# Attention of an audio tower: token tiles of 128 rows, and the last 64 tokens of two heads in one tile

## The chip, the cores and the metric

The kernel runs on one core of one Trainium2 chip. The metric is the device time of one execution in microseconds. Engines are named as in the profile: PE is TensorE (matrix products), PEld its weight loads, DVE is VectorE, ACT is ScalarE, POOL is GpSimd, and SP is the engine that issues the transfers.

## What is computed

Thirty-two sounds of 160,000 samples are cut into S = 313 frames of 512 samples. A discrete cosine transform gives the tokens h. One attention layer and one feed-forward layer follow, each with a normalisation ahead of it and a residual sum behind it. Everything is float32.

```python
h = einsum('bfh,kh->bfk', frames, D)
h = h + attn(layernorm(h))
h = h + ffn(layernorm(h))

def attn(X):                                   # H = 8 heads of 64
    Q = xpos(einsum('bsd,hde->bhse', X, W_Q), False)
    K = xpos(einsum('bsd,hde->bhse', X, W_K), True)
    V = einsum('bsd,hde->bhse', X, W_V)
    p = softmax(einsum('bhse,bhte->bhst', Q, K)) * Dmat      # Dmat = gamma_h ** |s - t|
    Y = einsum('bhst,bhte->bhse', p, V)
    Yn = group_norm(Y) * gn_weight + gn_bias                 # over each head's 64 values
    return silu(X @ W_G) * Yn @ W_O

def ffn(x):                                    # N = 256 units
    theta = x[..., None, :] / (1 + abs(W)) + B_param         # b, s, N, 512
    sin, cos = sine and cosine of theta, rounded to 4096 steps of the circle
    return silu(sum(cos * attn_cos) @ proj_cos.T + sum(sin * attn_sin) @ proj_sin.T)
```

The feed-forward layer takes a sine and a cosine of 32 x 313 x 256 x 512 angles each, which makes up most of the kernel.

## The kernel before

**Feed-forward.** Work goes in rounds of 32 units for a ring of up to 16 sequences. A slot holds 24 (sequence, unit, chunk of 128 features) pieces of 313 tokens, 7512 columns. For each slot DVE makes table indices (L665), adds a quarter turn (L674) and masks (L681); ACT takes two sines of 128x7512 (L689), each into one of two `trig` buffers; PE sums each of them over the features with 24 products against one-hot weights (L711), 32 output rows at a time. In the trace a float32 product leaves two records. The ring grows over the kernel: sequences join it at the rounds in `STARTS`, two at a time, so their attention has to be finished by then. At the beginning and the end the ring is narrow.

**Attention.** `attention()` computes one sequence. Its 313 tokens are cut into three tiles of N = 105 rows, which start every 104 rows (`ROW0` = 0, 104, 208), so neighbouring tiles share one token. The shared row of V is set to zero once (L362) so that it isn't counted twice. The steps, in order:
- `rows` (L296 to L308): a product of tokens with a 512x512 matrix, tokens as output rows. For each of four chunks `c` of the features three products, one for each row tile, into three banks of `W` in PSUM. It is used for the cosine transform, V, the output matrix, and once in `output` (L595).
- `layernorm`, then `transposed` (L285 to L294): 4 x 3 transposes on PE.
- `rotary` (L367): q and k of a pair of heads, by `columns` (L310), then L384 and L387 on DVE.
- `scores` (L391): for a pair of heads three row tiles; each has a product for either head (64 rows of contraction, 105 output rows, 313 columns, L401), the row maximum (L406) and the difference from it (L410) on DVE. The two products use different halves of the array's rows.
- the exponential on ACT (L427) in two halves of four heads, 4 x 3 x 313 = 3756 columns each, and its row sums on DVE (L442). For sequences 0, 1 and three more, when the ring is narrow, ACT does 24 exponentials of 313 columns, which sum their rows themselves (L431).
- per head: nine transposes of 105x105 (L457) into three banks, and the product with the decay on DVE (L469, 3 x 313 columns), with a decay table loaded for each head (L450) into one of the two halves of `u`. After every second head three pairs of products with V (L480; two heads in the two halves of the array's columns), and a copy (L486).
- the gate (L490 to L495), the sums of squares of each head (L515), the group norm's factor (L522 to L527, transposed in L532 and copied in L535), spread over the 64 features of a head by a product with `head_w` (L540), the output matrix and the second normalisation.

Sequences 0 and 1 run at the very start, side by side in two sets of buffers, `a` and `b`, and nothing else runs then. The other 30 run one after the other in `a`, between the feed-forward slots.

**What sets the order.** `Plan` (L52) takes every step with a key (when it is due), an engine, an assumed duration in ns, and what it reads and writes; `emit` walks through assumed time and, on each engine, takes the ready step of the lowest key. The program is emitted in that order, and each engine runs its own instructions in order. So a step that waits on PE holds up the feed-forward products behind it. Assumed durations that matter here: 970 for a product of `rows`, 400 for three transposes, 690 for a pair of score products, 610 for a product of the group norm.

**Buffers.** `prob` holds eight heads of three tiles (24 x 313 columns). Before the scores are in it, parts of it hold the table of the rotation, its products and other short-lived things; `W` has four banks.

## Time and profile before

| what | us |
|---|---|
| time, median of 3 runs | 18446.96 (18434.6 to 18453.94) |
| time of the profiled execution | 18427.45 |
| its span, first to last instruction | 18425.7 |
| mean granted TensorE clock | 0.924 |
| L689, 2758 sines | 17390.1 busy, 6391 ns each |
| L711, 131072 records | 10255.2 busy |
| L665, L681, L674 together | 15015.5 busy |
| L427, 54 exponentials of 105x3756 | 177.1 busy, 3327 ns each |
| L303 and its weight loads, 2160 + 840 records in `a` | 1436.0 and 482.8 busy |

A group of the profile gives the line, the engine and the operation, then what it writes and reads with the shape, how often it occurs, its busy time and the mean length of one. The time after the second bar is how long the engine stood idle just before instructions of the group, and what ended that. Records of PE overlap, so a mean length is longer than the pace; the pace is read from the timeline, where each stretch of equal instructions has a start, a length and a number.

### The profile page before, as it was taken

Reading aid. Unit: us, or ns where it says so; the run is one execution under the profiler, and the core shown is the slowest. Engines: PE = TensorE matmul, PEld = TensorE weight load, DVE = VectorE, ACT = ScalarE, POOL = GpSimd, SP = SyncE. Lnnn points to the kernel's source line nnn. Section 1 sums busy time; section 2 is a strip of 40 time slices with the busy share of each in tenths; the row PEclk is TensorE's granted clock in tenths of the full one; section 3 lists DMA queues with packets and bytes.
Section 4 is the critical chain, followed back from the end, with each engine's and each line's share of the span. In section 5 each row is a group of like instructions: output and inputs, shape, how many; then the busy total and the mean of one; then the engine's idle time right before and its main releaser. Section 6 shows DMA issues by size and latency. Waiting matters only on the chain. (4 is left out here: it accounts for less than half of the span.)

```text
span 18425.7 us, 322107 instructions
## 1 busy us (share of the span) xinstructions
PE 14166.8 (77%) x146432; PEld 6345.6 (34%) x146432; DVE 17099.8 (93%) x11554; ACT 17817.6 (97%) x3250; POOL 1268.7 (7%) x1118
## 2 busy tenths in 40 slices
PE   7888888777777787777787777877777777766666
PEld 4333334333333333333333333333333333322222
DVE  6999999999999999999999999999998999988888
ACT  4899999999999999999999999999999999999999
POOL 0011111010100010000101000010100000000000
PEclk8999999999999999999999999999999999998888
DMA  3221121111111111111111111111111111110101
GB/s 95 79 67 60 56 67 58 54 48 58 49 39 48 58 50 51 52 44 54 49 56 48 50 46 50 57 51 54 45 43 49 42 52 52 42 43 22 38 26 57
DMA packets 610376, 947.69 MB, mean 51 GB/s; under 512 B 123600, under 2 KB 348880, under 8 KB 598768
## 3 DMA queue, kind: packets, MB, share of 16 engines
q1 hardware_dynamic: 609008, 927.08, 16.4%
q8 instruction: 1148, 18.81, 0.4%
q14 instruction: 220, 1.80, 0.0%
HBM read 822.15 MB, written 104.66 MB: 50 GB/s over the span
## 5 line engine op out<-in xcount | busy, mean ns | idle before, releaser
L689 ACT ACTIVATE trig<-ix 128x7512 f32<-128x7512 int16 (+1 forms) x2758 | 17390.1, 6391 | 319.2 <-PE pa L711 178.8
L711 PE MATMUL pa<-trig,hot 128*32 128x313 f32 x131072 | 10255.2, 466 | 3630.8 <-ACT trig L689 3584.3
L711 PEld LDWEIGHTS pa<-trig,hot 128*32 128x32 f32 x131072 | 4274.7, 118 | 9500.3 <-ACT trig L689 4888.7
L665 DVE TENSOR_SCALAR ix<-xT,f 128x2504 int16<-128x2504 f32 (+3 forms) x5504 | 6531.3, 1247 | 120.0 <-ACT trig L689 58.8
L681 DVE TENSOR_SCALAR ix<-ix 128x15024 int16<-128x15024 int16 (+4 forms) x1655 | 5581.6, 3387 | 39.9
L674 DVE TENSOR_SCALAR ix<-ix 128x7512 int16<-128x7512 int16 (+1 forms) x1379 | 2902.6, 2105 | 646.2 <-ACT trig L689 558.7
L318 PE MATMUL a_W<-a_xnT,a_ring 128*128 128x313 f32 x4896 | 1455.8, 440 | 56.0 <-DVE a_prob L410 13.6
L303 PE MATMUL a_W<-a_ring,a_u 128*105 128x512 f32 x2160 | 1036.6, 618 | 93.4 <-ACT a_h L599 37.6
L318 PEld LDWEIGHTS a_W<-a_xnT,a_ring 128*128 128x128 f32 x4896 | 884.0, 190 | 631.9 <-issue 252.0
L250 POOL TENSOR_TENSOR a_gu<-a_gr 105x24 f32<-105x24 f32 x90 | 118.7, 1318 | 8753.3 <-DVE a_gr L238 8748.6
L303 PEld LDWEIGHTS a_W<-a_ring,a_u 128*105 128x105 f32 x2160 | 347.6, 174 | 661.4 <-issue 567.9
L250 POOL TENSOR_TENSOR a_lu<-a_lr 105x3 f32<-105x3 f32 x180 | 196.2, 1090 | 4870.7 <-DVE a_lr L238 4861.3
L457 PE MATMUL a_W<-ident,a_prob 105*105 105x105 f32 x2232 | 294.3, 276 | 194.7 <-DVE a_prob L469 155.1
L303 PE MATMUL a_W<-a_ring,a_xnT 128*105 128x512 f32 x840 | 399.4, 614 | 16.7 <-ACT a_h L599 6.5
L457 PEld LDWEIGHTS a_W<-ident,a_prob 105*105 105x105 f32 x2232 | 242.0, 180 | 338.5 <-DVE a_prob L469 147.9
L410 DVE TENSOR_TENSOR a_prob<-a_W,a_mx 105x626 f32<-105x626 f32 x372 | 301.2, 810 | 59.7 <-PE a_W L401 36.1
L406 DVE TENSOR_REDUCE a_mx<-a_W 105x2 f32<-105x626 f32 x372 | 298.4, 802 | 43.0 <-PE a_W L401 31.8
L401 PE MATMUL a_W<-a_u 64*105 64x313 f32 x1488 | 260.9, 457 | 80.7 <-DVE a_mx L406 56.3
L469 DVE TENSOR_TENSOR a_prob<-a_W,a_u 105x939 f32<-105x939 f32 x248 | 280.0, 1129 | 25.0 <-PE a_W L457 22.6
L480 PE MATMUL a_W<-a_prob,a_h 105*64 105x313 f32 x1488 | 241.9, 453 | 76.2 <-DVE a_prob L469 76.1
L384 DVE TENSOR_TENSOR a_prob<-a_W,a_prob 128x1252 f32<-128x1252 f32 x124 | 180.7, 1458 | 49.0 <-PE a_W L380 34.5
L442 DVE TENSOR_REDUCE a_sm<-a_prob 105x6 f32<-105x1878 f32 x108 | 220.3, 2101 | 0.0
(144 smaller groups left out, 3452.3 us busy)
## 6 DMA issues: line engine op xcount, KB each, us to landing
hot<-in_hot SPq DMA_DIRECT2D x1376, 128.0 KB
xT<-xT_d SPq DMA_DIRECT2D x80, 1252.0 KB
a_u<-in_decay SPq DMA_DIRECT2D x248, 260.5 KB
xT<-xT_d SPq DMA_DIRECT2D x36, 939.0 KB
a_ring<-in_proj SPq DMA_DIRECT2D x128, 256.0 KB
a_ring<-in_dct SPq DMA_DIRECT2D x124, 256.0 KB
a_ring<-wv_d SPq DMA_DIRECT2D x124, 256.0 KB
a_ring<-in_wq SPq DMA_DIRECT2D x124, 256.0 KB
```

Of the source, the lines that this page charges most:

```text
L250: nc.gpsimd.tensor_tensor(u, r, r, ALU.mult)
L303: lambda c=c, i=i, k=k, to=to: nc.tensor.matmul(x.W[:N, to, :], lhsT[:, c, ROW0[i] : ROW0[i] + N], x.ring[k], start=(c == 0), stop=(c == N ...
L318: lambda c=c: nc.tensor.matmul(x.W[:, bank, :S], w[:, c, :], x.xnT[:, c, :], start=(c == 0), stop=(c == NC4 - 1)),
L406: lambda b=b, m=m: nc.vector.tensor_reduce(m[:N], x.W[:N, b : b + 2, :S], AX.X, ALU.max),
L410: lambda i=i, b=b, m=m: nc.vector.tensor_tensor(x.prob[:N, 2 * g : 2 * g + 2, i, :], x.W[:N, b : b + 2, :S], m[:N].unsqueeze(2).to_broadca ...
L457: nc.tensor.transpose(x.W[:N, jj, ROW0[i] : ROW0[i] + N], x.prob[:N, a, i, ROW0[j] : ROW0[j] + N], ident[:N, :N],)
L469: nc.vector.tensor_tensor(x.prob[:N, a], x.W[:N, :NT, :S], w3, ALU.mult)
L665: nc.vector.tensor_scalar(ix[:, x[0], pt * r * S : (pt + 1) * r * S], now["xT", y][:, : r * S], f[:, 0, n : n + 1], f[:, 1, n : n + 1], AL ...
L674: nc.vector.tensor_scalar(ix[:, x[1], :E], ix[:, x[0], :E], float(LUT // 4), None, ALU.add)
L681: nc.vector.tensor_scalar(ix[:, i, :E], ix[:, i, :E], LUT - 1, LUT // 2, ALU.bitwise_and, ALU.bitwise_xor)
L689: nc.scalar.activation(tl[:, :E], ix[:, x[1 - k], :E], AF.Sin, bias=-PI32, scale=ANG)
L711: nc.tensor.matmul(now["pa", p][g * 32 : g * 32 + 32, :S], now["hot", hot[n // 4 * 4, c]][:, n % 4, k, :], now["trig", w][:, s0 : s0 + S], ...
```

## The change

The row tiles become two of 128 rows and one of 64: rows 0 to 127, 128 to 255 and 249 to 312. The last one starts at S - 64, so its first seven rows (`TWICE`) are tokens that the second tile has as well. In everything that has a token in each row, the third tile's 64 rows are computed twice, in the partitions 0 to 63 and 64 to 127. In what belongs to heads, the lower half belongs to the first head of a pair and the upper half to the second. A pair of heads thus has five tiles (two full ones per head, one shared) of 313 columns, where it had six.

- `rows` issues two products of 64 columns for the third tile; `transposed` a transpose of 64 rows. The residual is loaded in four parts, and so is the one in `output`.
- `scores` does two rounds for each pair, and `last_scores` one round for two pairs.
- The exponential covers 2 x 5 x 313 = 3130 columns for each half, and 20 single ones instead of 24 where ACT sums. The row sums are five of 4 x 313 columns instead of four of 6 x 313.
- In the heads, a decay table is loaded for a pair (1195 columns instead of 521 for a head), into `u` for even pairs and into a new place, `spare`, for odd ones. Two blocks of three transposes for each head fill two banks. The last 64 columns of both heads go to a third bank, by products with the identity (`both`). The decay is multiplied in three steps for a pair: 2, 2 and 1 times 313 columns.
- The third of the products with V uses 64 rows of contraction. L515's third tile has two groups of products, and the group norm's factor is spread with three products for each `c` instead of one.
- The scratch places within `prob` move: the rotation's table is in `spare`.

```diff
+LAST = 64
...
-    STEP = (S - 1) // NT
-    N = S - STEP * (NT - 1)
-    ROW0 = [i * STEP for i in range(NT)]
+    N = P
+    ROW0 = [0, P, S - LAST]
+    TWICE = 2 * P - ROW0[2]
+    WIN = S + P
...
+            wide = sb("prob", (5 * NC4 + 4) * S)
+            self.prob = wide[:, : 5 * NC4 * S].rearrange("p (g x s) -> p g x s", g=NC4, s=S)
+            spare = wide[:, 5 * NC4 * S :]
+            self.dec = [self.u.rearrange("p c s -> p (c s)")[:, : 2 * WIN + S],
+                        spare[:, : 2 * WIN + S]]
...
                 for i in range(NT):
+                    n = P if i < 2 else LAST
                     nc.tensor.transpose(
-                        x.W[:, c, ROW0[i] : ROW0[i] + N], x.h[:N, i, c * P : (c + 1) * P],
-                        ident[:N, :N],
+                        x.W[:, c, ROW0[i] : ROW0[i] + n], x.h[:n, i, c * P : (c + 1) * P],
+                        ident[:n, :n],
...
+                def go(c=c, i=i, k=k, to=to):
+                    for o in (0,) if i < 2 else (0, LAST):
+                        n = P if i < 2 else LAST
+                        nc.tensor.matmul(
+                            x.W[o : o + n, to, :], lhsT[:, c, ROW0[i] : ROW0[i] + n], x.ring[k],
+                            start=(c == 0), stop=(c == NC4 - 1))
+                plan.add(key, "PE", 970, go, (*r, x.k("ring", k)), x.banks(to))
...
+            for p0 in (0, LAST):
+                nc.gpsimd.memset(x.v[p0 : p0 + TWICE, 2], 0.0)
...
-            for i in range(NT):
-                b = (g * NT + i) % 2 * 2
+            for i in range(2):
+                b = turns[0] % 2 * 2
...
+        def last_scores(g):
+            key, b = step(), turns[0] % 2 * 2
+            def go():
+                for y in range(2):
+                    for a in range(2):
+                        r = slice(a * DH, a * DH + DH)
+                        nc.tensor.matmul(x.W[r, b + y, :S], x.qk[y][r, 0, ROW0[2] : S],
+                                         x.qk[y][r, 1, :], start=True, stop=True)
+            plan.add(key, "PE", 1240, go, us, x.banks(b, b + 1))
+            below_max(key, b, x.prob[:, g : g + 2, 4, :], (probs[g][4], probs[g + 1][4]))
...
+                    nc.scalar.activation(x.prob[:, g0 : g0 + 2], x.prob[:, g0 : g0 + 2], AF.Exp)
...
+            plan.add(key, "SP", DMA_NS,
+                     lambda g=g, dec=dec: nc.sync.dma_start(dec, t["decay"][g]), (), kd)
...
+            for a in range(2):
+                if a:
+                    key = step("head")
+                for jj in range(2):
+                    def go(g=g, a=a, jj=jj):
+                        k = slice((1 - jj) * P, (2 - jj) * P)
+                        for i in range(2):
+                            nc.tensor.transpose(x.W[:, jj, i * P : (i + 1) * P],
+                                                x.prob[:, g, 2 * i + a, k], ident)
+                        r = slice(a * LAST, a * LAST + LAST)
+                        nc.tensor.transpose(x.W[:, jj, ROW0[2] : S], x.prob[r, g, 4, k],
+                                            ident[r, r])
+                    plan.add(key, "PE", 400, go, [probs[g][y] for y in (a, 2 + a, 4)], x.banks(jj))
+                if a == 0:
+                    def both(g=g):
+                        k = slice(ROW0[2], S)
+                        for a in range(2):
+                            r = slice(a * LAST, a * LAST + LAST)
+                            for i in range(2):
+                                nc.tensor.matmul(
+                                    x.W[r, 2, i * P : (i + 1) * P], x.prob[:, g, 2 * i + a, k],
+                                    ident, start=True, stop=True)
+                            nc.tensor.matmul(x.W[r, 2, ROW0[2] : S], x.prob[r, g, 4, k],
+                                             ident[r, r], start=True, stop=True)
+                    plan.add(key, "PE", 600, both, probs[g], x.banks(2))
+                decayed(key, 2, x.prob[:, g, a : a + 3 : 2, :], 0, a * WIN, x.banks(0, 1),
+                        (probs[g][a], probs[g][a + 2]))
+            decayed(key, 1, x.prob[:, g, 4:5, :], 2, 2 * WIN, x.banks(2), (probs[g][4],))
...
+                        f = slice(b * DH, (b + 1) * DH)
+                        r = f if jj == 2 else slice(0, P)
+                        nc.tensor.matmul(
+                            x.W[f, 3, :S], x.v[r, jj, g, f],
+                            x.prob[r, g, 4 if jj == 2 else 2 * jj + b, :],
+                            start=(jj == 0), stop=(jj == NT - 1))
...
+            def spread(c=c):
+                nc.tensor.matmul(x.W[:, c, : 2 * P], x.head_w[:, 0, c, :], x.rT[:, : 2 * P],
+                                 start=True, stop=True)
+                for b in range(2):
+                    f = slice(b * DH, (b + 1) * DH)
+                    nc.tensor.matmul(x.W[f, c, ROW0[2] : S], x.head_w[:, 1, c, f],
+                                     x.rT[:, 2 * P + b * LAST : 2 * P + (b + 1) * LAST],
+                                     start=True, stop=True)
+            plan.add(key, "PE", 610, spread, probs[1], x.banks(c))
```

## The prediction

> **What bounds the kernel now.** I read the busy shares first, then busy time in stretches, then what the busiest engine waited for.
>
> ```profile
> PE 14166.8 (77%) x146432; PEld 6345.6 (34%) x146432; DVE 17099.8 (93%) x11554; ACT 17817.6 (97%) x3250; POOL 1268.7 (7%) x1118
> ```
>
> ScalarE works 97% of the span, so 608 us of it are idle. The stretches (columns: length, then busy time of PE, PEld, DVE, ACT, POOL) say where:
>
> ```profile
> 0.00:620.00 620.00, 476.69 (x3145) 244.42 (x3149) 448.79 (x609) 326.31 (x220) 22.21 (x43) 0.87 0.30 90
> 620.00:1240.00 620.00, 508.04 (x4743) 245.33 (x4739) 585.47 (x614) 557.56 (x197) 38.84 (x53) 0.92 0.25 74
> 1860.00:2480.00 620.00, 493.38 (x4976) 235.95 (x4969) 600.01 (x442) 584.39 (x103) 52.10 (x37) 0.93 0.18 56
> ...
> 6200.00:6820.00 620.00, 499.89 (x5161) 226.18 (x5155) 590.59 (x360) 617.44 (x103) 66.89 (x50) 0.93 0.15 48
> ```
>
> Four regimes. Until 306 us (the first L689 sine) only two attentions run, in a chain of PE, DVE and ACT. From there to about 3720 us DVE is the fullest engine (585 and 600 of 620). From 3720 us ACT is full (617 of 620). After 16120 us no attention runs. Nine sequences fall into the second regime (three before 1240 us, six after), 21 into the third, by the starts of L362, one per sequence. What ACT waited for:
>
> ```profile
> ACT trig L689 <- PE pa L711: 178.8, 101, 6.1
> ACT trig L689 <- DVE ix L681: 75.9, 33, 10.5
> ```
>
> By stretch, the wait for PE is 81 us in 300 to 1240, 47 us in 1240 to 3720, 40 us in 3720 to 17200. It is a sine that finds both `trig` buffers still being read by L711.
>
> The groups that the change touches:
>
> ```profile
> L410 DVE TENSOR_TENSOR a_prob<-a_W,a_mx 105x626 f32<-105x626 f32 x372 | 301.2, 810 | 59.7 <-PE a_W L401 36.1
> L406 DVE TENSOR_REDUCE a_mx<-a_W 105x2 f32<-105x626 f32 x372 | 298.4, 802 | 43.0 <-PE a_W L401 31.8
> L457 PE MATMUL a_W<-ident,a_prob 105*105 105x105 f32 x2232 | 294.3, 276 | 194.7 <-DVE a_prob L469 155.1
> L469 DVE TENSOR_TENSOR a_prob<-a_W,a_u 105x939 f32<-105x939 f32 x248 | 280.0, 1129 | 25.0 <-PE a_W L457 22.6
> L442 DVE TENSOR_REDUCE a_sm<-a_prob 105x6 f32<-105x1878 f32 x108 | 220.3, 2101 | 0.0
> ```
>
> **Two rules of the Trainium skill.** "TensorEngine Tiling (Array Packing)", Key Properties, says that work on separate parts of the array runs side by side, but that "Changing tiling mode (not just tile) drains the TensorE". The trace agrees, in PE's timeline of the start-up (start, length):
>
> ```profile
> 80.95 1.22 PE L380 MATMUL a_W<-a_prob,swap_m 128*128 128x313 f32 x4
> 82.00 2.80 PE L318 MATMUL b_W<-b_xnT,b_ring 128*128 128x313 f32 x10
> 84.73 1.30 PE L401 MATMUL a_W<-a_u 64*105 64x313 f32 x8
> 85.97 1.32 PE L380 MATMUL b_W<-b_prob,swap_m 128*128 128x313 f32 x4
> ```
>
> Inside one mode L380 takes 1.05 us for 4 records, 0.2625 each (every product leaves two). Ten L318 then fill 2.63 us, but L401 starts after 2.73; its eight half-array records, two at a time, fill 1.05, but L380 starts after 1.24. Out and back costs 0.1 + 0.19 = 0.29 us. I go by this number; the page gives none.
> "ScalarE: Activation LUTs", What ACT_TABLE_LOAD costs, prices an activation at 186 ns plus 0.833 ns per element: 3315 ns for L427's 3756 elements. The trace has 3327; the slope holds.
>
> **ACT.** L427 goes from 3756 to 3130 elements: 626 x 0.833 = 0.52 us, 54 times, 28 us; the 21 late sequences have 42 of them, 22 us, on the path, since ACT is full there. The five sequences whose exponentials are single activations go from 24 to 20, 0.45 us apart in the timeline: 1.8 us each.
>
> **DVE, per sequence.** L406 and L410 run 10 times for 12: 2 x (802 + 810) = 3.2 us. A row of n elements costs about 145 + 1.042 n ns (from L442). L442 becomes five of 1252, 1.45 us each, for four of 2.10: 1.15 us less. L469 becomes eight of 626 (0.81) and four of 313 (0.48), 8.4 for 9.0: 0.6 us less. L535 grows by 0.07. Together 4.9 us, or 3.8 where L442 doesn't run. In the second regime that is 3 x 3.8 + 6 x 4.9 = 41 us, at most what the time there falls by. Later DVE waits for ACT anyway, and it is worth nothing.
>
> **PE, per sequence.** The products are as many as before where one half tile stands for two heads, but they change mode far more often.
> - L303: the third row tile becomes two 64-column products side by side, no longer than the one they replace, with one trip out and back for each `c`: 4 x 4 calls (L595 among them) x 0.29 = 4.6 us.
> - L290: the third transpose has 64 rows: 4 x 2 calls, 2.3 us.
> - L457: 48 transposes for 72 at 0.12 us (nine in 1.08 us): 2.9 less; 16 trips: 4.6 more.
> - The 64-column blocks of `both` are products and not transposes: for each pair four of 128 columns (0.2 us: 0.525 x 128/313), two small ones and four changes of mode, 1.85 us: 7.4 in all.
> - L540 gets 4 trips, 1.2; L515 four more products, 0.5.
> Sum: 4.6 + 2.3 + 1.7 + 7.4 + 1.7, some 18 us more on 112. Low end 13 (trips at 0.2). High end 25: trips at 0.35, and half-row products into one bank (`last_scores`, the third Y product), which no row shows, not running side by side, 4 us.
>
> **Who pays.** An ACT sine takes 6.4 us and its L711 group 3.37, so about 3 us lie between groups for attention. Along the emitted order, with these prices, the gaps that hold more than 3 us go from 45 to 52 in the stretch from 300 us, from 56 to 76 from 1240 us, and from 43 to 123 from 3720 us; what they hold above 3 us goes from 80 to 103, 67 to 102 and 49 to 167 us: 176 us more. Such an excess needn't stop ACT: with two `trig` buffers PE may fall 3 us behind, and catches up in the next short gap. The mean excess from 3720 us on is 1.4 us, so only runs of long gaps count. Bounds: none of it, or as much as before, where ACT waited about 0.8 us for each us of excess. I take 0.2: 37 us, mostly where products of L303 follow each other.
> A `both` or transpose that waits for DVE holds up the L711 group behind it, and so ACT; that wait exists now (L457 for L469, 155 us) and there are as many hand-overs as before.
>
> **Start-up** (all on the path). From 86.1 to 116.8 us twelve rounds of L401, L406, L410 take 30.7 us, 2.56 each. Ten of them save 5.1, twice: 10 us. The four fewer activations save 2. The rows (6 calls x 1.16) cost 7, L290 (4 calls, some at half clock) 5; in the heads from 182 to 212 us PE is about 85% busy with six pairs: 2.1 x 6 x 0.8 = 10; the first two pairs 1, L540 and L515 3. Net +14 us; between +3 and +25.
>
> **Moves priced at nothing.** The decay loads are four of 612 KB for eight of 260 KB. The one into `u` waits for the pair two before; a whole pair lies between. If that cover failed, a few us per pair would be lost: the 626 KB load of the frames was late by at most 6.2 us. SP has four issues fewer and two more (a residual and an output row block each in two parts), and the DMA engines are 16% busy with its queue. The two POOL memsets replace one, on an engine 7% busy.
>
> **Sum.** Profiled execution: 18427.45 us, span 18425.7; the median of the runs is 18446.96, 19.5 above. Start-up +14; DVE's 41 at 80%, since PE and ACT share that regime, -33; ACT -22; late PE +37. Net -4 us: 18423 profiled, about 18443 for the median. No change. The measurement can tell about 0.2%, 37 us.
>
> **Rivals.**
> - *The gain comes through.* The drains hide in PE's waits for ACT (3056 us from 700 to 17000), no sine waits longer: start-up +3, -41, -22: -60, so 18387. For it: from 3720 us ACT runs without a break for tens of sines. Against it: PE is already the engine that ACT waits for most.
> - *PE becomes the late engine.* In the gaps between L711 groups the changes of mode push PE behind, and ACT loses 0.8 us per us of excess as before: 176 x 0.8 = 141, +14, -63: +92, 18540. For it: the early stretches have PE at 82% already, and `both` comes in one block. It decides once half of the 176 us reach ACT: 88 + 14 - 63 = 39, over 0.2%. Against it: the second buffer.
> - *Fewer tiles aren't less work*: nothing of DVE's saving shows, since ACT paces everything: +14 - 22 + 37 = +29, 18476. It lies inside the first case's range, 18410 to 18485.
>
> **Chances.** No change 0.37 (with the last rival; 0.28 of it within 0.2%, 0.05 faster, 0.04 slower), gain 0.31 (0.29 faster, 0.02 within), PE late 0.32 (0.31 slower, 0.01 within). Faster 0.34, same 0.31, slower 0.35. The range reaches into both others: 18365 to 18550; the likeliest's own is 18410 to 18485.
>
> **What would show it.** L427 near 2.8 us; L442's successor 1.45 us; DVE busy down by about 150 us (31 x 4.9); PE busy up by 400 to 800 us, with gaps around the half-array products; the first sine near 320 us; ACT's wait for L711 from 179 to about 215 us. If that wait stays, the gain is there; if it passes 270, PE decides. Wrong altogether: a decay load that DVE waits for, or a mode change dearer than 0.35 us.

## The result, and the profile after

The changed kernel takes 18555.19 us (median of 5 runs, 18533.01 to 18563.57) against 18446.96 before: the ratio is 1.0057, with a 95% interval of 1.0043 to 1.0072. It is slower by 108 us, where no change was forecast, and 5 us above the range. Its profiled execution took 18546.98 us with a span of 18545.2, 119.5 more than before.

The sizes of the work came out nearly as forecast. The line of busy times after:

```profile
PE 14649.4 (79%) x148992; PEld 6440.8 (35%) x148992; DVE 16942.9 (91%) x11581; ACT 17788.7 (96%) x3210; POOL 1267.1 (7%) x1150
```

DVE has 157 us less, ACT 29 less, PE 483 more, 15.1 for each of the 32 sequences. The groups (L404 and L407 are L406 and L410 of before, L454 is L427, L471 is L442, L492 is L469, L502 and L505 are L457, L514 and L517 are `both`):

```profile
L407 DVE TENSOR_TENSOR a_prob<-a_W,a_mx 128x626 f32<-128x626 f32 x310 | 250.9, 809 | 71.2 <-PE a_W L436 37.4 <-PE a_W L422 25.1
L404 DVE TENSOR_REDUCE a_mx<-a_W 128x2 f32<-128x626 f32 x310 | 248.4, 801 | 32.7 <-PE a_W L436 25.7 <-PE a_W L422 6.3
L502 PE MATMUL a_W<-ident,a_prob 128*128 128x128 f32 x992 | 236.9, 324 | 213.3 <-DVE a_prob L492 198.8 <-ACT a_prob L454 13.7 <-DVE a_h L537 0.6
L514 PE MATMUL a_W<-ident,a_prob 128*64 128x128 f32 x992 | 163.6, 288 | 4.1 <-DVE a_h L537 4.1
L471 DVE TENSOR_REDUCE a_sm<-a_prob 128x4 f32<-128x1252 f32 x108 | 151.5, 1448 | 0.0
L454 ACT ACTIVATE a_prob<-a_prob 128x3130 f32<-128x3130 f32 x54 | 149.0, 2807 | 0.3
L505 PE MATMUL a_W<-ident,a_prob 64*128 64x64 f32 x496 | 143.0, 288 | 0.0
L492 DVE TENSOR_TENSOR a_prob<-a_W,a_prob 128x626 f32<-128x626 f32 x124 | 99.6, 803 | 5.7 <-PE a_W L505 4.8 <-PE a_W L517 0.8
```

128 rows cost DVE what 105 did (801 and 809 ns), and each exponential is 0.52 us shorter. The four stretches, with the columns of before:

```profile
0.00:620.00 620.00, 503.74 (x3153) 242.10 (x3157) 406.85 (x570) 297.97 (x193) 23.45 (x36) 0.86 0.29 87
620.00:1240.00 620.00, 527.60 (x4791) 242.60 (x4791) 574.59 (x627) 543.19 (x178) 54.04 (x64) 0.94 0.26 78
1860.00:2480.00 620.00, 515.31 (x5101) 240.66 (x5093) 589.81 (x441) 583.32 (x102) 59.39 (x40) 0.94 0.19 57
6200.00:6820.00 620.00, 499.30 (x5080) 218.00 (x5078) 575.82 (x356) 605.99 (x103) 61.51 (x50) 0.93 0.16 50
```

In the last of them ACT, which was full with 617 us, has 606. ACT's waits in the whole execution (L749 is the sine, L771 the products that read `trig`):

```profile
ACT trig L749 <- PE pa L771: 240.0, 138, 6.0
ACT trig L749 <- issue: 104.5, 45, 8.5
ACT trig L749 <- DVE ix L741: 69.3, 25, 14.3
```

The first row was 178.8 us. The second, 54.2 before, belongs with it: in the places looked at below, the sine starts right after a late group of L771, and the view names no releaser. The two together went from 233 to 345 us.

Both kernels take the same 2758 sines, so the starts of equal sines (counted from 0), after minus before, say where the time came from. The first is 21.0 us late; the 100th (1064 us in the kernel before) 34.2; the 491st (3734 us) 31.5; the 2400th (16107 us) 114.9. So 21 us lie in the start-up; 10 in the regime where DVE was fullest, where 33 us of gain had been forecast; and 83 in the late one, where the forecast had 22 us of gain and at most 37 of loss. In the late one, from 3734 to 16200 us, ACT's idle time ahead of sines (gaps over 0.3 us), its stalls, went from 65.6 to 162.0 us.

Between the first and the 491st sine DVE works 40 us less, as forecast, but is idle for 50 us more. The largest new wait is that of the copy behind the heads, for which the view names the products of `both` ahead of it on PE. In that stretch it is 12 us before and 38 after. The rows of the whole execution, before and after:

```profile
L486 DVE COPY a_h<-a_W 128x313 f32<-128x313 f32 x124 | 59.6, 481 | 56.9 <-PE a_W L457 47.1 <-PE a_W L318 8.2 <-PE a_W L480 1.3
L537 DVE COPY a_h<-a_W 128x313 f32<-128x313 f32 x124 | 59.9, 483 | 162.6 <-PE a_W L517 148.3 <-PE a_W L322 9.0 <-PE a_W L505 3.1
```

Three of PE's waits in the late stretch (from 3817 to 16200 us), out of a longer list:

```profile
PE a_W L502 <- DVE a_prob L492: 127.6, 55, 8.0
PE a_W L309 <- DMA a_u<-in_frames: 44.3, 9, 6.0
PE a_W L586 <- POOL a_gr L257: 31.8, 11, 4.2
```

The same three were 71.0, 21.3 and 25.9 us before. How such a wait reaches ACT is seen in the timeline of after (start, length, then the instructions; the time in brackets is the wait ahead):

```profile
12247.55 0.80 PE L586 MATMUL a_W<-ident,a_gr 128*8 128x128 f32 x3 [4.10 <-POOL a_gr L257]
12248.99 1.22 PE L594 MATMUL a_W<-a_prob 8*128 8x256 f32 x2 [0.64 <-DVE a_prob L589]
12250.13 0.48 PE L598 MATMUL a_W<-a_prob 8*64 8x64 f32 x4
12250.54 1.22 PE L594 MATMUL a_W<-a_prob 8*128 8x256 f32 x2
12252.09 6.14 PE L771 MATMUL pa<-trig,hot 128*32 128x313 f32 x48
12258.16 0.69 PE L594 MATMUL a_W<-a_prob 8*128 8x256 f32 x2
12258.36 6.47 ACT L749 ACTIVATE trig<-ix 128x7512 f32<-128x7512 int16 x1 [5.63 <-issue]
```

After 4.10 us of waiting PE runs at about half pace: L594 takes 1.22 us there and 0.69 later, the group of L771 6.14 us instead of 3.37. Two of the four spread steps (L594 and L598, with their changes of mode 3.1 us together) stand ahead of that group, and ACT stops for 5.63 us. In the kernel before, the same place has a wait of 2.52 us, one product ahead of the group, and ACT doesn't stop:

```profile
12155.59 0.43 PE L532 MATMUL a_W<-ident,a_gr 105*8 105x105 f32 x3 [2.52 <-POOL a_gr L253]
12156.59 0.79 PE L540 MATMUL a_W<-a_prob 8*128 8x313 f32 x2 [0.57 <-DVE a_prob L535]
12157.31 5.06 PE L711 MATMUL pa<-trig,hot 128*32 128x313 f32 x48
```

The trace also records the clock that PE was granted. It is half of full speed from 12247.5 to 12257.7 us after, and from 12158.2 to 12161.6 before. The Trainium skill ("TensorE: Matmul & The Clock Gate", Part 1) puts the half clock behind an idle window of about 3.4 us. The wait of 4.10 us agrees; before, the waits of 2.52 and 0.57 us with products between them were enough. The price is that of these timelines: 5.06 and 6.14 us for 3.37.

How much of the loss goes with this half clock? From 3734 to 16200 us it holds for 1635 us before and 1707 after, so there is hardly more of it. But 64 of the 66 us of stalls before, and 156 of the 162 after, come when more than 2 of the 14 us ahead of the sine were at half clock, which is so for 40% of all sines there. In the other twelve kernels below, it is 85 to 100% of the stalls. And the time in which PE worked for the attention at half clock went from 69 to 155 us. So the added work seems to stop ACT where it meets the half clock. No run changes the clock alone, so that is a reading of the traces and not shown by experiment.

### The profile page after: what moved, and what is told of

Read it like the earlier page. It is cut to its first block, busy times and chain, and to the rows that moved or that the text cites. A ratio compares the mean times of both kernels' runs of the same rounds, so it can differ in the third digit from the quotient of the medians.

```text
span 18545.2 us, 327113 instructions
## 1 busy us (share of the span) xinstructions
PE 14649.4 (79%) x148992; PEld 6440.8 (35%) x148992; DVE 16942.9 (91%) x11581; ACT 17788.7 (96%) x3210; POOL 1267.1 (7%) x1150
## 3 DMA queue, kind: packets, MB, share of 16 engines
q1 hardware_dynamic: 595632, 946.67, 16.7%
## 5 line engine op out<-in xcount | busy, mean ns | idle before, releaser
L749 ACT ACTIVATE trig<-ix 128x7512 f32<-128x7512 int16 (+1 forms) x2758 | 17398.6, 6392 | 438.9 <-PE pa L771 240.0
L771 PE MATMUL pa<-trig,hot 128*32 128x313 f32 x131072 | 10240.5, 466 | 3212.4 <-ACT trig L749 3156.8
L771 PEld LDWEIGHTS pa<-trig,hot 128*32 128x32 f32 x131072 | 4273.3, 118 | 9044.8 <-ACT trig L749 4355.4
L309 PE MATMUL a_W<-a_ring,a_u 128*64 128x512 f32 (+1 forms) x2880 | 1120.8, 635 | 117.5 <-DMA a_u<-in_frames 48.2
L309 PEld LDWEIGHTS a_W<-a_ring,a_u 128*64 128x64 f32 (+1 forms) x2880 | 320.0, 165 | 788.2 <-issue 675.7
L254 POOL TENSOR_TENSOR a_lu<-a_lr 128x3 f32<-128x3 f32 x180 | 201.5, 1119 | 4970.1 <-DVE a_lr L242 4894.6
L309 PE MATMUL a_W<-a_ring,a_xnT 128*128 128x512 f32 (+1 forms) x1120 | 422.9, 622 | 9.7 <-ACT a_h L659 3.4
L502 PE MATMUL a_W<-ident,a_prob 128*128 128x128 f32 x992 | 236.9, 324 | 213.3 <-DVE a_prob L492 198.8
L407 DVE TENSOR_TENSOR a_prob<-a_W,a_mx 128x626 f32<-128x626 f32 x310 | 250.9, 809 | 71.2 <-PE a_W L436 37.4
L404 DVE TENSOR_REDUCE a_mx<-a_W 128x2 f32<-128x626 f32 x310 | 248.4, 801 | 32.7 <-PE a_W L436 25.7
L531 PE MATMUL a_W<-a_prob,a_h 128*64 128x313 f32 x1488 | 255.0, 459 | 16.4 <-DVE a_prob L492 16.3
L422 PE MATMUL a_W<-a_u 64*128 64x313 f32 x992 | 179.3, 472 | 70.4 <-DVE a_mx L404 59.0
L502 PEld LDWEIGHTS a_W<-ident,a_prob 128*128 128x128 f32 x992 | 106.7, 150 | 345.9 <-DVE a_prob L492 225.0
L309 PEld LDWEIGHTS a_W<-a_ring,a_xnT 128*128 128x128 f32 (+1 forms) x1120 | 122.7, 163 | 263.6 <-issue 241.8
## 6 DMA issues: line engine op xcount, KB each, us to landing
a_prob<-in_decay SPq DMA_DIRECT2D x62, 597.5 KB
a_u<-in_decay SPq DMA_DIRECT2D x62, 597.5 KB
```

What stands on the lines that cost most here:

```text
L254: nc.gpsimd.tensor_tensor(u, r, r, ALU.mult)
L309: nc.tensor.matmul(x.W[o : o + n, to, :], lhsT[:, c, ROW0[i] : ROW0[i] + n], x.ring[k], start=(c == 0), stop=(c == NC4 - 1))
L404: lambda: nc.vector.tensor_reduce(m, x.W[:, b : b + 2, :S], AX.X, ALU.max),
L407: lambda: nc.vector.tensor_tensor(place, x.W[:, b : b + 2, :S], m.unsqueeze(2).to_broadcast((P, 2, S)), ALU.subtract),
L502: nc.tensor.transpose(x.W[:, jj, i * P : (i + 1) * P], x.prob[:, g, 2 * i + a, k], ident)
L531: nc.tensor.matmul(x.W[f, 3, :S], x.v[r, jj, g, f], x.prob[r, g, 4 if jj == 2 else 2 * jj + b, :], start=(jj == 0), stop=(jj == NT - 1))
```

## The experiments

The columns: median, how much it lies above that of the kernel before, and the ratio to it; PE's busy time over that of before; then, in the profiled execution against the one of before, when the first, the 491st and the 2400th sine start, and the span; last, ACT's late stalls (3734 to 16200 us; 65.6 before). A stall is put down to the product, or the wait ahead of one, that took most of PE in the 14 us before the sine, the sums of the sines not counted. Single profiled executions stray by 10 us and more (that of `turns_whole` lies 23 us below its median), and PE's busy time by some 50: before_late does the same work as the kernel before. The kernel before was timed beside each set of kernels: 18446.96 us beside after, 18438.4 beside the four rows below it, 18444.6 beside the next four, 18445.9 beside the last four. So kernels of different sets are compared by the column "above".

| kernel | median, us | above | ratio (95%) | PE | first | 491st | 2400th | span | stalls |
|---|---|---|---|---|---|---|---|---|---|
| after | 18555.2 | +108.2 | 1.0057 (1.0043 to 1.0072) | +483 | 21.0 | 31.5 | 114.9 | 119.5 | 162.0 |
| rows_whole | 18523.4 | +85.0 | 1.0043 (1.0030 to 1.0055) | +426 | 13.3 | 3.3 | 82.7 | 84.1 | 153.9 |
| turns_whole | 18511.1 | +72.8 | 1.0041 (1.0027 to 1.0054) | +338 | 2.2 | -9.9 | 58.3 | 60.3 | 146.0 |
| whole_tiles | 18437.9 | -0.4 | 1.0000 (0.9992 to 1.0008) | +160 | -1.1 | -29.1 | 11.3 | 10.5 | 120.5 |
| plan_told | 18472.4 | +34.0 | 1.0017 (1.0009 to 1.0025) | +391 | 20.5 | 25.2 | 55.4 | 56.6 | 118.4 |
| before_split | 18445.6 | +1.0 | 1.0002 (0.9993 to 1.0010) | +130 | 7.8 | 16.7 | 19.8 | 24.8 | 66.8 |
| before_late | 18428.5 | -16.1 | 0.9991 (0.9982 to 0.9999) | +54 | 5.9 | 12.4 | 2.4 | 2.8 | 49.6 |
| best_whole | 18392.4 | -52.2 | 0.9971 (0.9960 to 0.9983) | +122 | -7.8 | -31.6 | -38.5 | -38.3 | 76.1 |
| best_late | 18369.7 | -74.9 | 0.9959 (0.9946 to 0.9971) | +145 | 1.0 | -16.2 | -56.0 | -51.3 | 44.1 |
| after_spread | 18508.1 | +62.2 | 1.0036 (1.0024 to 1.0049) | +454 | 14.3 | 7.1 | 86.0 | 91.1 | 154.0 |
| after_both | 18520.2 | +74.2 | 1.0043 (1.0031 to 1.0056) | +409 | 20.7 | 20.1 | 85.0 | 92.5 | 144.9 |
| after_frames | 18541.5 | +95.6 | 1.0053 (1.0040 to 1.0065) | +513 | 26.2 | 42.8 | 106.6 | 111.2 | 143.3 |
| best_start | 18350.7 | -95.2 | 0.9952 (0.9939 to 0.9966) | +97 | -9.1 | -27.0 | -78.2 | -76.8 | 36.9 |

The theory after the result: the changes of mode and the slow `both` make PE late, and the plan makes it worse, since it orders the work with durations that hold none of this (400, 600, 610 and 970 ns are unchanged). The rivals: the new order alone, one of the visible waits, or the half clock behind waits, whatever PE's work is.

**rows_whole.** The third row tile as one product of 128 columns, tokens 185 to 312:

```diff
-                    for o in (0,) if i < 2 else (0, LAST):
-                        n = P if i < 2 else LAST
-                        nc.tensor.matmul(
-                            x.W[o : o + n, to, :], lhsT[:, c, ROW0[i] : ROW0[i] + n], x.ring[k],
-                            start=(c == 0), stop=(c == NC4 - 1))
+                    r0 = ROW0[i] if i < 2 else S - P
+                    nc.tensor.matmul(x.W[:, to, :], lhsT[:, c, r0 : r0 + P], x.ring[k],
+                                     start=(c == 0), stop=(c == NC4 - 1))
```

> The third row tile of every rows product is one product of 128 columns (tokens 185 to 312) instead of two of 64, in the same instruction order; the lower half of that tile then holds other tokens, so this leaves out the doubled tokens of V. It takes away 16 of the 44 changes of tiling mode of a sequence and 16 products. Theory 1 (changes of mode make PE late, and ACT loses about 0.8 us for each us): 16 x 0.29 = 4.6 us of 18 per sequence, so a quarter to a third of the 108 us comes back: 18520 to 18530. Theory 2 (the planner's new order puts a few blocks badly, at L586/L594 and at the first L309 after the frames' load, whatever PE's work is): 18545 to 18555, since the order is the same. Theory 3 (PE goes cold in waits and the group behind it runs at half clock): 18545 to 18555 too.

The lower half of the third tile then holds tokens 185 to 248 where later steps take it for 249 to 312. So the doubled tokens are left out, here and in whole_tiles.

Measured: 23 us less above its before than after is, and the intervals of the two ratios overlap. PE's busy time falls by only 57 us, and the first sine comes 8 us earlier, against 7 us priced for these rows.

**turns_whole.** The transposes of 64 rows become transposes of 128. In the heads they go first, and the second full tile then takes 121 rows, so that it covers what belongs to the other head:

```diff
-                    n = P if i < 2 else LAST
...
-                        x.W[:, c, ROW0[i] : ROW0[i] + n], x.h[:n, i, c * P : (c + 1) * P],
-                        ident[:n, :n],
-                    )
+                        x.W[:, c, ROW0[i] : ROW0[i] + P], x.h[:, i, c * P : (c + 1) * P], ident)
...
+                        o = ROW0[2] - a * LAST
+                        nc.tensor.transpose(x.W[:, jj, o : o + P], x.prob[:, g, 4, k], ident)
...
-                            nc.tensor.transpose(x.W[:, jj, i * P : (i + 1) * P],
-                                                x.prob[:, g, 2 * i + a, k], ident)
-                        r = slice(a * LAST, a * LAST + LAST)
-                        nc.tensor.transpose(x.W[:, jj, ROW0[2] : S], x.prob[r, g, 4, k],
-                                            ident[r, r])
+                            n = P if i == 0 else ROW0[2] - P
+                            nc.tensor.transpose(x.W[:, jj, i * P : i * P + n],
+                                                x.prob[:n, g, 2 * i + a, k], ident[:n, :n])
```

> The transposes of 64 rows (L295 and the third of each three in the heads) become transposes of 128 rows, in the same instruction order; nothing is left out. It takes away 24 of the 44 changes of mode. Theory 1: 24 x 0.29 = 7 us of 18 per sequence, some 40 us back: 18505 to 18520. Theories 2 and 3: 18545 to 18555.

Measured: 35 us less above its before than after is, PE 145 us less, and most of the start-up's loss is gone (21.0 to 2.2): there these transposes lie on the path.

**whole_tiles.** Both edits, and the products of `both` in the order shown under after_both.

> Both of the edits before, and in both() the products of 64 columns of the two heads next to each other so that they run side by side, then the two small ones (2 changes of mode instead of 4, and half the time of the products). Same order; the doubled tokens of V are left out as in rows_whole. Together 4.6 + 7 + 2.8 = 14 of PE's 18 us per sequence. Theory 1: most of the loss goes, 18440 to 18470, PE busy near 14200. Theory 2 or 3: over 18530, with ACT's waits for L771 still near 240 us though PE is less busy.

Measured: 1.0000. With 323 of the 483 us of PE's extra work gone, the loss is gone, and the early gain appears: from the first sine to the 491st the time falls by 28 us. But the late stretch still loses 40 us against before, with stalls of 120.5 us. So PE's extra work, changes of mode and the products of `both` together, is one cause, not the only one. The half clock behind waits, whatever PE's work is, had put this kernel over 18530; that theory falls.

**plan_told.** The instructions of after; only the plan's durations are changed:

```diff
-            plan.add(key, "PE", 400, go, x.rows_of, x.banks(c))
+            plan.add(key, "PE", 650, go, x.rows_of, x.banks(c))
-                plan.add(key, "PE", 970, go, (*r, x.k("ring", k)), x.banks(to))
+                plan.add(key, "PE", 970 if i < 2 else 1250, go, (*r, x.k("ring", k)), x.banks(to))
-                    plan.add(key, "PE", 400, go, [probs[g][y] for y in (a, 2 + a, 4)], x.banks(jj))
+                    plan.add(key, "PE", 700, go, [probs[g][y] for y in (a, 2 + a, 4)], x.banks(jj))
-                    plan.add(key, "PE", 600, both, probs[g], x.banks(2))
+                    plan.add(key, "PE", 1900, both, probs[g], x.banks(2))
-            plan.add(key, "PE", 610, spread, probs[1], x.banks(c))
+            plan.add(key, "PE", 950, spread, probs[1], x.banks(c))
```

> The same instructions as the changed kernel, but the planner is told what the pieces take: 1250 for the third row tile, 650 and 700 for three transposes, 1900 for both, 950 for a spread. Only the order changes. Theory 1: PE's work is the same, so little comes back, 18530 to 18560. Theory 2: the order is the cause, and an order made with true durations brings half or more back, 18440 to 18500. Theory 3: between, if PE waits less often for POOL, DVE and DMA.

Measured: 74 us less above its before than after is, with the same work, where the theory of PE's work alone had little coming back. So the order is a second cause. That it is the right durations, and not only another order, is likely and not shown: orders changed by one load's landing alone moved the time by 13 and 16 us (after_frames, before_late), and none was made with arbitrary durations. In the late stretch PE was at half clock for 1484 us and not 1707, which goes with its lower busy time. The start-up, where nothing can be put between, stays at 20.5; the late stretch loses 30 us instead of 83. The stalls beside the spread fall from 36 to 9 us; 89 of the 118 that are left stand beside L309, 35 of them at its wait for the frames.

**before_split.** The kernel before, its third row product cut in two on the two halves of the array:

```diff
+                def go(c=c, i=i, k=k, to=to):
+                    for o, n in ((0, N),) if i < 2 else ((0, 64), (64, N - 64)):
+                        nc.tensor.matmul(
+                            x.W[o : o + n, to, :], lhsT[:, c, ROW0[i] + o : ROW0[i] + o + n],
+                            x.ring[k], start=(c == 0), stop=(c == NC4 - 1))
+                plan.add(key, "PE", 970, go, (*r, x.k("ring", k)), x.banks(to))
```

> The kernel before with each product of the third row tile in two, of 64 and 41 columns, on the two halves of the array: 16 trips out and back of the tiling mode per sequence, nothing else changed, and the same order of the plan. If changes of mode by themselves cost time: PE busy up by 31 x 16 x 0.2 to 0.29 = 100 to 145 us, and 20 to 60 us slower, part of it at the start (8 to 16 trips a sequence on the path). If only the order that was made with the 128-row tiles costs time: PE busy up the same, the time within 10 us of the kernel before.

Measured: no slower (1.0002), where 20 to 60 us were expected if changes of mode cost time by themselves; the late stretch takes 3 us more. Three row products between two groups of sums, as they stand most often, in the timelines of the kernel before and of before_split:

```profile
8239.60 2.82 PE L303 MATMUL a_W<-a_ring,a_u 128*105 128x512 f32 x6
```

```profile
8257.00 2.97 PE L303 MATMUL a_W<-a_ring,a_u 128*105 128x512 f32 x8
```

A trip out and back costs 0.15 us here: by estimate 2.4 us for the 16 of a sequence and 77 us for all 32. Such a small dose of changes of mode, in the order of before, hides.

**before_late and best_late.** The plan is told that the frames' load lands 4 us later than its 2.5 us, in the kernel before and in best_whole:

```diff
+        self.late = {}
...
+            more = self.late.get(i, 0.0)
-            end = t + dur + (self.LAND if e == "SP" else 0.0)
+            end = t + dur + (self.LAND + more if e == "SP" else 0.0)
...
+        plan.late[len(plan.ops)] = 4000.0
         plan.add(step(), "SP", DMA_NS, lambda: nc.sync.dma_start(x.u, t["frames"][sq]), (), us)
```

> The kernel before with only that statement on the frames' load. If this wait costs what PE's wait for it shows (21 us after 3734 us, of which ACT loses about 0.8): 10 to 25 us faster, 18415 to 18430. If it only moves work about: within 8 us of the kernel before, and any gain of best_late belongs to the tiles of 128 rows.

> The kernel of best_whole, with one more statement: the planner is told that the frames' load lands 4 us later than other loads, so that it puts the first row products behind another sine's group. Rival of best_whole (frames' load is a late wait of its own, 35 us in plan_told): 10 to 30 us below best_whole, and PE's wait for the frames after 3734 us from some 35 to 40 us down to under 10. Theory 1 alone: within 10 us of best_whole, because PE would have been late in these places anyway.

Measured: before_late is 16 us faster; its interval just excludes 1. best_late is 23 us below best_whole; among the longest waits of PE after 3700 us that for the frames (45.3 us in best_whole) is not found any more. At the first sine they are 6 and 9 us later than their bases, which is no more than single executions stray by.

**best_whole.** The idea of whole_tiles without the loss of V's doubled tokens, where only V takes the split products (`twice`), and with two things learnt from the traces: durations for the plan, and a spread in two kinds of step, the second with all 64-column products:

```diff
+    ROWS = [0, P, S - P]
...
+                    if i < 2 or not twice:
+                        nc.tensor.matmul(x.W[:, to, :], lhsT[:, c, ROWS[i] : ROWS[i] + P], x.ring[k],
+                                         start=(c == 0), stop=(c == NC4 - 1))
+                        return
-                plan.add(key, "PE", 970, go, (*r, x.k("ring", k)), x.banks(to))
+                plan.add(key, "PE", 1250 if twice and i == 2 else 970, go, (*r, x.k("ring", k)), x.banks(to))
...
-                    plan.add(key, "PE", 600, both, probs[g], x.banks(2))
+                    plan.add(key, "PE", 1000, both, probs[g], x.banks(2))
...
+            plan.add(key, "PE", 500, lambda c=c: nc.tensor.matmul(
+                x.W[:, c, : 2 * P], x.head_w[:, 0, c, :], x.rT[:, : 2 * P],
+                start=True, stop=True), probs[1], x.banks(c))
+        plan.add(key, "PE", 900, spread, probs[1], x.banks(0, 1, 2, 3))
```

> Nothing of the computation is left out. Tiles of 128 rows as in the kernel after, but no work is done on half tiles that a whole tile can do: the third row tile is tokens 185 to 312 as 128 rows (only V keeps its doubled 64 tokens), the head transposes of the shared tile are taken as 128 rows, both() is put in order so that products of one mode follow each other, the spread runs in two steps, and the planner is told durations that contain the remaining changes of mode. Theory 1 (the loss was changes of mode plus an order made without knowing of them): PE's busy time within 200 us of the kernel before, ACT's stalls from 3734 us back to 65 to 90 us, and the savings of DVE and ACT come out: 18390 to 18425, ratio 0.997 to 0.999. Rival (the late loss lies in the frames' load and the spread, which stay): the early gain of 29 us is there, 40 us are lost late, 18430 to 18450, ratio 0.999 to 1.000.

Measured: 18392.4, as the theory expected. Here stalls can be set side by side, as a table of two by two: few changes of mode and a plan that knows them 76 us (best_whole); many changes, told 118 (plan_told); few, not told 120 (whole_tiles); many, not told 162 (after). In these single executions the two causes add, some 43 us each. In the whole time they do so less evenly: by the column "above", the plan is worth 74 us with many changes and 52 with few, the fewer changes 109 and 86. It isn't a pure pair, because best_whole also differs from whole_tiles in V's split products, in the residual's loads (three parts for four) and in the spread's two kinds of step: beside the spread, stalls are 34 us in whole_tiles and 5 in best_whole, so most of the second cause shows at that one place.

**after_spread, after_both, after_frames.** One place of after mended at a time: the spread as in best_whole; the frames' landing as in best_late; and

```diff
                     def both(g=g):
-                        for a in range(2):
-                            r = slice(a * LAST, a * LAST + LAST)
-                            for i in range(2):
+                        half = [slice(a * LAST, a * LAST + LAST) for a in range(2)]
+                        for i in range(2):
+                            for a, r in enumerate(half):
                                 nc.tensor.matmul(
                                     x.W[r, 2, i * P : (i + 1) * P], x.prob[:, g, 2 * i + a, k],
                                     ident, start=True, stop=True)
+                        for r in half:
                             nc.tensor.matmul(x.W[r, 2, ROW0[2] : S], x.prob[r, g, 4, k],
```

> The kernel after, with one place mended: the spread over the heads' rows in two kinds of step (four products of 256 columns, then all eight 64-column products in one step), 4 trips of the tiling mode a sequence become one, and the planner is told their durations. The trace of after puts 36 us of ACT's late stalls beside the spread and its wait for POOL. If the late loss is made of a few places: 25 to 40 us below after, 18515 to 18530. If lateness is one sum over the whole attention, which shows wherever PE happens to be behind: the 3 us fewer of PE's 15.6 per sequence are worth about a fifth of the loss at most, and the stall appears elsewhere: 18535 to 18555.

> The kernel after with the six products of both() in another order, so that products of one mode follow each other: 1.67 us each becomes about 0.85, 3.3 us per sequence less on PE (100 us of its busy time), no change of the plan. No stall of after is put beside both(). A few places: within 10 us of after. One sum: a fifth of the loss, 20 to 25 us below after, 18530 to 18537.

> The kernel after, with one place mended: the planner is told that the frames' load lands 4 us later. The trace of after puts 26 us of ACT's late stalls beside PE's wait for this load. A few places: 15 to 30 us below after, 18525 to 18540. One sum: within 10 us of after; in the kernel before the same edit gave a ratio of 0.9991.

Measured: 46, 34 and 13 us less above before than after is; the last is within the intervals. The first two are more than either theory said. after_spread's is mostly early: by the profiled executions 7 us before the first sine and 18 more up to the 491st. Late it is worth 5 us; beside the spread the stalls fall from 36 to 13, and two thirds of that come back elsewhere. after_both gained 18 us late, though next to no stall had stood beside `both`. So a stall in this kernel is where PE's lateness shows, and not always where it arises. A part of after before the reordering, and the same part of after_both:

```profile
12102.69 0.65 PE L514 MATMUL a_W<-ident,a_prob 128*64 128x128 f32 x4
12103.27 0.33 PE L517 MATMUL a_W<-ident,a_prob 64*64 64x64 f32 x2
12103.53 0.65 PE L514 MATMUL a_W<-ident,a_prob 128*64 128x128 f32 x4
12104.11 0.33 PE L517 MATMUL a_W<-ident,a_prob 64*64 64x64 f32 x2
```

```profile
12080.49 0.66 PE L514 MATMUL a_W<-ident,a_prob 128*64 128x128 f32 x8
12081.08 0.33 PE L518 MATMUL a_W<-ident,a_prob 64*64 64x64 f32 x4
```

Eight records take what four did: products for the two halves of the array overlap when they follow each other, and not when two for the same half come first. 1.75 us become 0.92.

**best_start.** best_late with the later landing told from the third sequence on only:

```diff
-        plan.late[len(plan.ops)] = 4000.0
+        if sq > 1:
+            plan.late[len(plan.ops)] = 4000.0
```

> The kernel of best_late with the later landing told from the third sequence on only, so that the two sequences of the start-up keep best_whole's order. best_late lost 8.8 us against best_whole before the first sine and gained 16 after 3734 us; if the two belong to different sequences, both are had: 18355 to 18364. If the order after the start-up depends on the order before it: 18365 to 18390.

Measured: 18350.7, 95 us below before; after was 108 above it. Its busy times and ACT's waits:

```profile
PE 14264.2 (78%) x148224; PEld 6423.9 (35%) x148224; DVE 16942.1 (92%) x11581; ACT 17778.9 (97%) x3210; POOL 1245.0 (7%) x1150
```

```profile
ACT trig L758 <- PE pa L780: 161.4, 86, 6.4
ACT trig L758 <- issue: 50.2, 15, 7.6
ACT trig L758 <- DVE ix L750: 45.0, 22, 6.3
```

DVE and ACT work as long as in after, to 1 and 10 us. What differs is ACT's wait for PE, 212 us in the first two rows for 345. Before_late has the same information on the frames but for the start-up. Against it, the tiles of 128 rows, with their plan and their spread, are worth 79 us.

## Why the prediction was wrong

- **DVE and ACT work: right in size.** L454 2.81 us (forecast 2.8), L471 1.448 (1.45), DVE 157 us less (150), ACT 29 less (37: 28 by L427 and 9 by the five sequences). But its worth did not come through. DVE's saving was to give 33 us from the first sine to the 491st; the kernel after loses 10 there. In whole_tiles and best_whole, with less work on PE, this stretch is 28 and 24 us shorter than before (13 of the 28 are less work of ACT).
- **PE's extra work: right in sum.** 15.1 us per sequence where 18 was forecast, with 13 as the low end. Three transposes with one of 64 rows take 0.57 us from start to next start, 0.2 more than whole ones; `both` takes 1.75 for 1.85. The trips of the row products were too dear (0.15 us in before_split for the 0.29 of the start-up).
- **Start-up: mis-sized.** +21.0 for +14, inside its bounds. rows_whole takes 8 us of it away (7 forecast), the spread 7 (L540 and L515 together were put at 3), turns_whole 19.
- **"I take 0.2": the step that failed.** PE's work in the gaps beyond 3 us each, the excess, was forecast to grow by 176 us, 118 of them late, and a fifth of it to stop ACT, because the second `trig` buffer lets PE fall 3 us behind and catch up. ACT's stalls grew by 118 us from the first sine on, 96 of them late. Of the excess as forecast that is 0.67, and 0.8 late: the upper bound, which was the ratio read from the kernel before. The 0.2 itself was read from no row.
- **The excess was also too small.** In the traces, PE's busy time between two groups of sums, beyond 3 us each, went from 57 to 221 us late and from 190 to 260 us ahead of that: 234 us in all for the 176. Measured against this, half of it stopped ACT. Of the two errors the share is the larger: 0.2 of 234 would be 47 us.
- **What the mean left out.** That PE catches up in the next short gap, since "the mean excess from 3720 us on is 1.4 us", takes the gaps to be spread evenly and PE to be at full pace. But the plan fills the gaps with what it takes for full: told of the added time, it left 152 us of late excess for 221, with as much work on PE, and saved 44 of the 96 us. And nearly all late stalls, 156 of 162 us, follow a stretch at half clock, in which a group takes up to 6.14 us for 3.37 and leaves 0.3 of a sine's 6.4.
- **The early regime.** There the same cost met DVE: its idle time grew by 50 us, 26 of them at the copy behind `both`, and took the 40 us that it works less.
- **The hand-overs, priced at nothing.** PE's late wait for DVE in the heads (L502 for L492) did grow, from 71.0 to 127.6 us. But best_start, the fastest kernel, has 200 us of it from 3700 to 16050 us, with stalls of 36.9, so this wait by itself isn't what stops ACT.
- **The rival "PE becomes the late engine"**, 18540, is what happened, 15 us short, 7 of them in the start-up. It was given 0.32, against 0.37 for no change. That the number comes so near is in part luck: it had 141 us more of stalls, where 118 came, and 41 us of gain by DVE, which did not come. Its condition, half of the 176 us reaching ACT, was met: from the first sine on ACT's stalls grew by 118 us. The mark for it, a wait for L771 over 270 us, was too narrow: that row reads 240, and the rest of the growth is in the row of "issue".
- **The decay loads and the POOL memsets** were priced at nothing; neither stands among the longest waits. (The sizes of the decay loads were put in two units: the view has 597.5 KB for a pair and 260.5 KB for a head.)
- What stays open: which share of the stalls the wrong durations cause at places other than the spread, since whole_tiles and best_whole differ in both; how far the half clock is a cause and not only a companion of the stalls, since no run changes it alone; and whether another order could hide all 483 us.

## What to carry to other kernels

Where an order is made from assumed durations, a change that makes instructions dearer must change these numbers too: the same instructions gave a ratio of 1.0057 with the old ones and 1.0017 with better ones. A row product was worth splitting over two parts of the array only where a later step needs the same tokens in both halves (here V alone), and products of one mode are better put together. An engine's slack, summed over a kernel, says little about whether more work on it hides: some 77 us, by the estimate from before_split, hid on an engine with 4200 us of idle time and 483 us didn't. The kernel before had shown the ratio, 0.8 us of stall for each us of excess; a share well below what the trace shows needs a reason of its own.

## What the runs showed of the hardware

- The price of a trip out of a tiling mode and back depends on the company: 0.15 us among row products, about 0.2 among transposes (three take 0.57 us with one of 64 rows), 0.29 between the start-up's products. This fits the drain that the skill names ("TensorEngine Tiling (Array Packing)", Key Properties).
- Products of 64 columns shared the array when those for the two halves stood next to each other (0.66 us for eight records). With two for the same half first, four records took 0.65 us.
- Behind a wait of 4.1 us the granted clock was half for 10.2 us, from 12247.5 to 12257.7, up to the end of the group that followed. Behind waits of 2.52 and 0.57 us it was half for 3.4 us, from 12158.2 to 12161.6.
